# Four attention and mixture-of-experts layers on one core: expert results scattered to token rows, read by plain loads, with a stepped end and a first batch that goes ahead

## The chip, the cores and the metric

The kernel runs on one core of a Trainium2 chip. The metric is the device time of one launch in microseconds (us). The engines are PE (matrix products and transposes), DVE, ACT and POOL (element-wise work; POOL also issues indirect DMAs), and SP, which only issues DMAs.

## The reference, cut to what matters

A state `x` of 2 x 512 tokens by 256 values goes through four layers. Each adds an attention to a context and then a mixture of experts. Everything is float32. In layers 2 and 3 every token goes to two of eight experts, and the two results are weighted and added (`_layernorm` stands ahead of each):

```python
x = x + _L2_xattn_ref(_layernorm(x), ctx_1024, ...)   # causal, 16 heads of 16
# layer 2, experts: 2 of 8, gates = softmax over the two logits
for e in range(NUM_EXPERTS):
    h = jax.nn.relu(jnp.einsum('bsd,fd->bsf', x, w1[e]))
    y = jnp.einsum('bsf,df->bsd', h, w2[e])
    out = out + combine[..., e, None] * y
x = x + _L3_xattn_ref(_layernorm(x), ctx_1024, ...)   # rotary, 16 heads of 16
# layer 3, experts: 2 of 8, on h = rmsnorm(x @ W_in.T, in_norm_w)
for e in range(Wg.shape[0]):
    oe = rmsnorm(jax.nn.silu(h @ Wg[e].T) * (h @ Wu[e].T) @ Wd[e].T, enorm_w[e])
    out = out + gates[:, e:e + 1] * oe
s_hat = rmsnorm(out, out_norm_w) @ W_out.T
```

Layers 0 and 1 send each token to one expert. The kernel computes a token only in the experts it goes to.

## The kernel before

The 1024 tokens are `TT = 8` tiles of 128 (partition = token). `X`, 128 x 8 x 256, holds the state on the chip all the time. Tiles 0 to 3 are batch 0, 4 to 7 batch 1.

**Experts (`moe`).** `slots_of` gives every pick of a token a slot: a row of the DRAM tensor `xd`. Slots come in tiles of 128, each tile for one expert: one tile per expert (`s < 8`) and further ones for what overflows. For each pick and each token tile POOL issues an indirect DMA that scatters the 128 rows to their slots (L415; 16 of them in layers 2 and 3). Then `slot_tile(s)` runs for each tile: it loads the expert's weights `w` (a plain load by SP, L429, for `s < 8`; a gather by POOL, L431, beyond; `bufs=4`, so the load for tile s waits until tile s-4 is done with its weights), the rows `xs` (SP, L438), turns them (PE, L446; copy to `sT` on DVE, L448), multiplies (L132, L456 to L463), multiplies again into `y` (L466), and `finish` writes `yo`: a copy on ACT in layer 2 (`plain`, L480), a root-mean-square scaling on ACT and DVE in layer 3 (`normalise`, L1470). ACT then stores `yo` to the rows of the tile's slots in `yd` (L469). 19 tiles always run in layer 2 and 21 in layer 3 (`ALWAYS`); the rest stand in a `tc.If` on the counted number of tiles, which is a branch on each engine (L474). In the profiled execution it isn't taken in these layers.

**Combine.** For each token tile and each pick POOL gathers the rows of `yd` that the tile's tokens need (L487), and DVE multiplies by the gate and adds (L494, L496), into `X` in layer 2, into `acc` in layer 3. A gather waits for the stores of `yd`. In layer 3 follow, for all eight token tiles: `rms` (sums of squares on ACT, one root, eight scalings on DVE, L1449), the transposes (`to_T`, L117, copies on ACT, L122), the product with `w_out` (`po`, L132), the add into `X` (L1487) and the store (L1488).

**Attention of layers 2 and 3 (`attend16`).** Keys and values were computed before (`ahead16`, into the DRAM tensors `kd` and `vd`; L512, L557 to L562) and `fetch` loads them. `into_xT` normalises all of `X` (statistics L72, L73; `recip_sqrt`, L61 to L63; L98), turns it (L1190, copies alternately on ACT and DVE, L185 and L183) and adds the output bias to `X` (`add_bias`, L179). `prep(n)` makes the queries of group n (four heads of one batch; groups 0 to 3 are batch 0), `rotate` (L147 to L149) turns the keys in layer 3. After that comes a stream of slots whose order on PE is written out (`pe_in_order`): scores for the row maxima (`first_pass`, L1210, the maxima on DVE, L1216 or L1220), and, ten or more slots behind, scores again with the maxima taken off (`second_pass`, L1267, exponentials on ACT, L1268) and the products with the values. `Pieces` is a list of generators that are advanced a step at a time between slots; it holds the queries of the next group and the output products.

**What sets the order.** Code is written in program order, and a scheduler then orders each engine's instructions by readiness and program order and adds the waits; it may move an instruction ahead of others. What `keep` or `pe_in_order` marks stays in order. Instructions in a `tc.If` aren't mixed with those outside. Each engine works through its own list in order, and a waiting instruction holds those behind it.

`fill_slots` writes zeros to `xd` and to the tiles of `yd` that the branch may skip, during layer 0's attention.

Of the kernel before, what the change touches and what calls it, by code (L numbers as in the profile page):

```python
# [10 lines left out]
F32 = mybir.dt.float32  # L11
I32 = mybir.dt.int32
AF = mybir.ActivationFunctionType
ALU = mybir.AluOpType
# [3 lines left out]
P = 128  # L18
# [15 lines left out]
def tile_kernel(ctx: ExitStack, tc: tile.TileContext, d: dict, out: bass.AP):  # L34
# [369 lines left out]
    def moe(L, ps, hp, ep, rows, slots, wrow, used, F, act, glu, finish, filler=None):  # L404


        n_over = wrow.shape[1]
        NS = E + n_over
        FT, W1 = F // P, (2 * F if glu else F)
        xd, yd = xds[L]  # L410

        put = []
        for si in slots:
# [12 lines left out]
        def slot_tile(s):  # L426
# [41 lines left out]
            finish(yo, y, w)  # L468
            nc.scalar.dma_start(yd[s * P : (s + 1) * P, :], yo)  # L469

# [10 lines left out]

    def combine(hp, yd, slots, gates, dst, first):

        for t in range(TT):
            for i, si in enumerate(slots):
                yg = hp.tile([P, D], F32, tag="yg", name="yg", bufs=8)
                nc.gpsimd.indirect_dma_start(  # L487
                    out=yg, out_offset=None, in_=yd, in_offset=bass.IndirectOffsetOnAxis(ap=si[:, t : t + 1], axis=0)
                )
                to = dst[:, t, :]  # L490
                if gates is None:
                    nc.vector.tensor_add(to, to, yg)
                elif first and i == 0:
                    nc.vector.tensor_scalar(to, yg, gates[i][:, t : t + 1], None, ALU.mult)  # L494
                else:
                    nc.vector.scalar_tensor_tensor(to, yg, gates[i][:, t : t + 1], to, ALU.mult, ALU.add)  # L496
# [101 lines left out]
    def fill_slots(ins):  # L598

        zeros = const.tile([P, D], F32, tag="zeros", name="zeros")  # L600
# [5 lines left out]
        for L, NS in (("L0", 15), ("L1", 15), ("L2", 23), ("L3", 23)):  # L606
            xds[L] = [dram.tile([NS * P, D], F32, tag=f"{L}{n}d", name=f"{n}d") for n in "xy"]
            for to in xds[L][0], xds[L][1][(E + ALWAYS[L]) * P :, :]:
                nc.gpsimd.dma_start(
                    to.rearrange("(s p) f -> p s f", p=P), zeros[:, None, :].to_broadcast([P, to.shape[0] // P, D])  # L610
                )
# [4 lines left out]

    def normed(pool, twice, tag="xn"):
        xn = pool.tile([P, TT, D], F32, tag=tag, name="xn")
        layernorm(xn, X, TT, twice)
        return xn  # L620
# [3 lines left out]
    with (  # L624
# [31 lines left out]
        c_iota = route[:, 120:240].rearrange("p (s e) -> p s e", e=E)  # L656
        c_base, c_first, c_part = route[:, 240:248], route[:, 248:256], route[:, 256:257]

        nc.gpsimd.tensor_scalar(sin, sin, sign[:, 0:1], None, ALU.mult)
# [216 lines left out]
    with (  # L876
# [27 lines left out]
        ahead1(ps, hp, wkv, cT, 1)  # L904
        combine(hp, yd, slots, [mp], X, False)

# [207 lines left out]
    def attend16(L, params, nkt, causal, rotary, bias):  # L1114
# [11 lines left out]
        with (  # L1126
# [56 lines left out]

            def into_xT():
                xn = normed(cp, False, "oT1")
                for blk in range(TT // 4):
                    for dc in range(2):
                        pt = bank("pt")
                        for i in range(4):
                            nc.tensor.transpose(  # L1190
                                pt[:, i * P : (i + 1) * P], xn[:, blk * 4 + i, dc * P : (dc + 1) * P], ident
                            )
                        copy_alt(dc, xT[:, dc, blk * 512 : (blk + 1) * 512], pt)
                add_bias(bo)
# [168 lines left out]
    with (  # L1363
# [28 lines left out]
        ahead16(ps, fp, "L2", params, 4)  # L1392
        combine(hp, yd, slots, None, X, False)

# [4 lines left out]
    with (  # L1399
# [6 lines left out]
        xT = fp.tile([P, 2, NT], F32, tag="xT", name="xT")  # L1406
        xn = normed(fp, False)
        to_T(ps, xT, xn, TT)
# [15 lines left out]
    with (  # L1424
# [16 lines left out]

        def rms(t, w):

            ss = small.tile([P, TT], F32, tag="ss8", name="ss8")
            for i in range(TT):
                mean_squares(ss[:, i : i + 1], t[:, i, :])
            r = recip_sqrt(ss, TT, 1.0 / D, RMS_EPS)
            for i in range(TT):
                nc.vector.scalar_tensor_tensor(  # L1449
                    t[:, i, :], t[:, i, :], r[:, i : i + 1], w, ALU.mult, ALU.mult  # L1450
                )

        xT = fp.tile([P, 2, NT], F32, tag="xT", name="xT")
        to_T(ps, xT, normed(fp, False), TT)
        h = fp.tile([P, TT, D], F32, tag="h", name="h")
        for t in range(TT):
            ph = ps.tile([P, D], F32, tag="mm", name="ph")
            mm2(ph, xT, slice(t * P, (t + 1) * P), w_in, slice(0, D))
            nc.scalar.copy(h[:, t, :], ph)
        rms(h, inw)  # L1460
        hnT = fp.tile([P, 2, NT], F32, tag="hnT", name="hnT")
# [19 lines left out]
        aT = fp.tile([P, 2, NT], F32, tag="xT", name="aT")  # L1481
        to_T(ps, aT, acc, TT)
        outv = out.flatten_outer_dims()
        for t in range(TT):
            po = ps.tile([P, D], F32, tag="mm", name="po")
            mm2(po, aT, slice(t * P, (t + 1) * P), w_out, slice(0, D))
            nc.vector.tensor_add(X[:, t, :], X[:, t, :], po)  # L1487
            nc.sync.dma_start(outv[t * P : (t + 1) * P, :], X[:, t, :])  # L1488

# [49 lines left out]
def _route():  # L1539

    e = np.arange(E, dtype=np.float32)
    row = np.concatenate([
# [5 lines left out]
    ]).astype(np.float32)  # L1548
    return np.concatenate([np.tile(row, (P, 1)), np.arange(P, dtype=np.float32)[:, None]], axis=1)

# [105 lines left out]
```

## Time and profile before

| | us |
|---|---|
| median of 3 runs (2302.83 to 2308.51) | 2302.84 |
| the profiled execution | 2307.93 |
| its span, first to last instruction | 2306.2 |
| PE busy / share of the span | 2094.5 / 91% |
| DVE busy / share | 1070.3 / 46% |
| ACT busy / share | 863.9 / 37% |
| POOL busy / share | 439.8 / 19% |
| layer 1's end and layer 2's first queries | 1222 to 1258 |
| layer 2's slot tiles behind the key work | 1480 to 1622 |
| layer 2's end and layer 3's first queries | 1622 to 1664 |
| layer 3's attention | 1664 to 1950 |
| layer 3's slot tiles | 2022 to 2263 |
| layer 3's end | 2263 to 2306 |

All times inside the span count from its first instruction. A row of the timeline gives start, duration, engine, line, operation, the tile written and those read, shapes, how many instructions are merged into it, and in brackets the idle time of the engine before it with what ended it. `SPq`, `ACTq` and `POOLq` are DMA issues and other instructions that don't count as busy. A float32 product appears as two matmuls, a transpose as one.

### The profile page before, as it was taken

The page shows a single profiled execution, that of the slowest core. Times are in us where ns is not written, and L with a number is a line of the kernel's source. Part 1 is how long each engine was busy: PE and PEld are TensorE (multiplying, and loading weights), DVE is VectorE, ACT ScalarE, POOL GpSimd, SP SyncE. Part 2 cuts the span into 40 slices and gives each one's busy share as a digit, 9 for nine tenths or more (in the row PEclk, how much of TensorE's full clock was granted, in tenths as well). Part 3 has the DMA queues.
Part 4 walks back from the last instruction along what each step waited for, and adds up shares of the span by engine and source line. Part 5 has one row for each costly group of instructions (what it writes and reads, how often), then busy time and mean ns, then how long its engine had stood idle before and what let it go on. Part 6 is the DMA issues. An engine that isn't in the chain of part 4 may idle for free. (4 is left out here: it accounts for less than half of the span.)

```text
span 2306.2 us, 30582 instructions
## 1 busy us (share of the span) xinstructions
PE 2094.5 (91%) x11892; PEld 1274.1 (55%) x11892; DVE 1070.3 (46%) x2017; ACT 863.9 (37%) x1652; POOL 439.8 (19%) x418
## 2 busy tenths in 40 slices
PE   7899999989998999998998998899399999489994
PEld 3344444459974445544685344699243333489993
DVE  7566666641125565555214772000477773212222
ACT  4344444431115655554111332312035555234332
POOL 3233222210012112111101221200423310200002
PEclk9999999999999999999898997999689999689997
DMA  6511111277844011003274115686311101557851
GB/s 189 174 33 42 33 29 31 88 273 277 308 147 137 28 37 37 28 1 123 86 256 137 34 30 228 239 310 241 106 51 47 34 15 70 212 214 308 325 221 60
DMA packets 105766, 301.93 MB, mean 131 GB/s; under 512 B 23504, under 2 KB 67792, under 8 KB 96912
## 3 DMA queue, kind: packets, MB, share of 16 engines
q1 hardware_dynamic: 72400, 155.57, 19.7%
q0 software_dynamic: 12384, 114.70, 13.4%
q10 hardware_dynamic: 20832, 29.63, 3.5%
q8 instruction: 98, 1.61, 0.3%
q14 instruction: 52, 0.43, 0.1%
HBM read 243.39 MB, written 48.41 MB: 127 GB/s over the span
## 5 line engine op out<-in xcount | busy, mean ns | idle before, releaser
L1268 ACT ACTIVATE p<-s 128x512 f32<-128x512 f32 (+3 forms) x384 | 185.9, 545 | 191.4 <-PE s L1267 130.5
L132 PE MATMUL pa<-sT,w 128*128 128x128 f32 x1920 | 236.2, 278 | 12.1 <-DVE sT L448 3.7
L132 PEld LDWEIGHTS pa<-sT,w 128*128 128x128 f32 x1920 | 227.4, 193 | 20.6 <-ACT sq L1440 5.8
L1210 PE MATMUL s<-kT,qT 32*128 32x512 f32 (+3 forms) x768 | 216.7, 612 | 13.1 <-POOL kT L149 6.1
L466 PE MATMUL y<-w,hT 128*128 128x256 f32 x960 | 219.6, 381 | 3.9 <-DVE hT L463 3.1
L1267 PE MATMUL s<-qA,kT 32*128 32x512 f32 (+3 forms) x768 | 198.8, 595 | 1.0 <-ACT p L1268 0.7
L466 PEld LDWEIGHTS y<-w,hT 128*128 128x128 f32 x960 | 177.3, 190 | 27.9 <-DVE hT L463 4.4
L1220 DVE TENSOR_REDUCE mx<-s 128x1 f32<-128x512 f32 x256 | 163.1, 684 | 54.4 <-PE s L1210 34.2
L463 DVE TENSOR_TENSOR hT<-act,pg 128x512 f32<-128x512 f32 x82 | 56.3, 688 | 266.3 <-PE pg L132 225.1
L132 PE MATMUL pg<-sT,w 128*128 128x128 f32 x1312 | 160.8, 276 | 1.0 <-ACT sv L529 1.0
L819 ACT ACTIVATE p<-s 128x1024 f32<-128x1024 f32 x128 | 124.2, 1021 | 98.1 <-PE s L814 98.0
L978 ACT ACTIVATE p<-s,nm 128x512 f32<-128x512 f32 x192 | 129.3, 685 | 82.8 <-DVE nm L975 82.8
L132 PEld LDWEIGHTS pg<-sT,w 128*128 128x128 f32 x1312 | 154.0, 193 | 1.2 <-ACT sv L529 1.2
L975 DVE TENSOR_REDUCE nm<-s 128x2 f32<-128x1024 f32 x96 | 113.2, 1221 | 81.9 <-PE s L971 81.8
L820 DVE TENSOR_SCALAR p<-p 128x1024 f32<-128x1024 f32 x128 | 106.6, 840 | 89.9 <-ACT p L819 89.9
L149 POOL TENSOR_TENSOR kT<-kT,turned 128x512 f32<-128x512 f32 x62 | 100.9, 1632 | 217.9 <-DVE turned L147 208.5
L448 DVE COPY sT<-pt 128x256 f32<-128x256 f32 x66 | 25.6, 419 | 246.1 <-PE pt L446 246.1
L745 PE MATMUL o<-p,v 128*64 128x512 f32 x512 | 126.4, 610 | 10.3 <-DVE p L820 10.3
L825 DVE TENSOR_TENSOR acc<-acc,p 128x1024 f32<-128x1024 f32 x96 | 133.8, 1394 | 2.8
L814 PE MATMUL s<-qT,kT 64*128 64x512 f32 x512 | 128.4, 620 | 0.0
L431 POOL DMA_INDIRECT w<-in_L_experts_dram,wrow x34 | 32.3, 950 | 501.5 <-PE pt L446 124.9
L1210 PEld LDWEIGHTS s<-kT,qT 32*128 32x128 f32 x768 | 78.2, 190 | 68.6 <-issue 26.1
(274 smaller groups left out, 3077.8 us busy)
## 6 DMA issues: line engine op xcount, KB each, us to landing
w<-in_L_experts_dram SPq DMA_DIRECT2D x8, 3200.0 KB
w<-in_L_experts_dram SPq DMA_DIRECT2D x8, 3072.0 KB
w<-in_L_experts_dram SPq DMA_DIRECT2D x8, 2048.0 KB
w<-in_L_experts_dram SPq DMA_DIRECT2D x8, 1536.0 KB
kd<-sk ACTq DMA_DIRECT2D x40, 256.0 KB
xs<-xd SPq DMA_DIRECT2D x66, 128.0 KB
yd<-yo ACTq DMA_DIRECT2D x66, 128.0 KB
kT<-kd SPq DMA_DIRECT2D x16, 512.0 KB
```

The source lines that it names most:

```text
L132: nc.tensor.matmul(ps_ap, lhsT[:, dc, lcols], rhs[:, dc, rcols], start=(dc == 0), stop=(dc == 1))
L466: nc.tensor.matmul(y, hT[:, f, :], w2[:, f, :], start=(f == 0), stop=(f == FT - 1))
L745: nc.tensor.matmul(G[n]["o"][64 * j : 64 * j + 64, :], V[g, b][:, kt, pr * P + 64 * j : pr * P + 64 * j + 64], p[:, j, :], start=(kt == 0) ...
L814: nc.tensor.matmul(s1[:, j, :], G[n]["kT"][r, kt * P : (kt + 1) * P], G[n]["qT"][r, :], start=True, stop=True)
L819: nc.scalar.activation(p, s1, AF.Exp, scale=0.125)
L825: nc.vector.tensor_add(G[n]["acc"], G[n]["acc"], p)
L975: nc.vector.tensor_reduce(nm[:, qt, :, c], s1, AX.X, ALU.max, negate=True)
L978: nc.scalar.activation(p[:, j, :], s1[:, j, :], AF.Exp, bias=nm[:, qt, j, c : c + 1], accum_out=l[:, qt, j, c : c + 1],)
L1210: nc.tensor.matmul(s1[:, :w], qT[r, qt * P : (qt + 1) * P], kT[r, c * 512 : c * 512 + w], start=True, stop=True)
L1220: nc.vector.tensor_reduce(mx[:, qt, j, c : c + 1], s1, AX.X, ALU.max)
L1267: nc.tensor.matmul(s2[:, qs], kT[r, kt * P : (kt + 1) * P], qA[r, qs], start=True, stop=True)
L1268: nc.scalar.activation(p[:, j, qs], s2[:, qs], AF.Exp, scale=0.25)
```

## The change

Four edits:

1. **Names travel with the rows.** In layers 2 and 3 the rows scattered to `xd` get a 257th value: the token's number `c_tok` (0 to 1023) for the first pick, `c_tok + 1024` for the second, written by DVE (one copy, and eight small adds between the scatters). Unused slots are filled with `2048 + partition`. `c_tok` is eight further columns of the constant `route`.
2. **Scatter instead of store.** Each slot tile turns its names into row numbers (three small DVE instructions) and POOL scatters `yo` to rows of `yd`: rows 0 to 1023 hold the first picks by token, 1024 to 2047 the second, and behind them lies a row for each unused slot (2048 + 128 s + partition). ACT's store goes in these layers. `yd` isn't filled with zeros there any more.
3. **Plain loads and steps.** `combine2` reads whole token tiles of `yd` with loads by SP: in layer 2 four tiles of one pick per load (four loads, batch 0 first), in layer 3 two tiles per load. Layer 3's end runs in four steps of two token tiles, each from the loads to the store. Layers 0 and 1 keep gathers and `combine`.
4. **One batch first.** In `attend16` (layers 2 and 3) the statistics, the normalising and the transposes are done for batch 0, then the first queries; the statistics of batch 1 are written ahead of the stream, and its normalising, transposes and the bias add become a generator in `Pieces`.

The diff's core:

```diff
@@ moe
+        named = len(slots) == 2
+        RW = D + named
+        for i, si in enumerate(slots):
+            if named and i == 0:
+                nc.vector.tensor_copy(rows[:, :, D], c_tok)
             for t in range(TT):
+                if i == 1:
+                    nc.vector.tensor_scalar(rows[:, t, D:], c_tok[:, t : t + 1], float(NT), None, ALU.add)
                 x = nc.gpsimd.indirect_dma_start(
...
-            xs = hp.tile([P, D], F32, tag="xs", name="xs", bufs=4)
+            xs = hp.tile([P, RW], F32, tag="xs", name="xs", bufs=4)
...
-            nc.scalar.dma_start(yd[s * P : (s + 1) * P, :], yo)
+            if not named:
+                nc.scalar.dma_start(yd[s * P : (s + 1) * P, :], yo)
+                return
+            to = hp.tile([P, 2], F32, tag="to", name="to", bufs=3)
+            nc.vector.tensor_scalar(to[:, 0:1], xs[:, D:], 2.0 * NT, float(s * P), ALU.is_ge, ALU.mult)
+            nc.vector.tensor_add(to[:, 1:2], to[:, 0:1], xs[:, D:])
+            ti = hp.tile([P, 1], I32, tag="ti", name="ti", bufs=3)
+            nc.vector.tensor_copy(ti, to[:, 1:2])
+            x = nc.gpsimd.indirect_dma_start(
+                out=yd, out_offset=bass.IndirectOffsetOnAxis(ap=ti[:, 0:1], axis=0), in_=yo, in_offset=None
+            ).ins
+            for y in out_of:
+                tc.declare_no_dep(x, y, reason="rows of different tokens")
+            out_of.append(x)
@@
+    def combine2(hp, yd, gates, dst, t0, n, first):
+
+        for i in range(2):
+            yg = hp.tile([P, n, D], F32, tag="yg", name="yg", bufs=4)
+            r0 = i * NT + t0 * P
+            nc.sync.dma_start(yg, yd[r0 : r0 + n * P, :].rearrange("(t p) f -> p t f", p=P))
+            for t in range(n):
+                to, g = dst[:, t0 + t, :], gates[i][:, t0 + t : t0 + t + 1]
+                if first and i == 0:
+                    nc.vector.tensor_scalar(to, yg[:, t, :], g, None, ALU.mult)
+                else:
+                    nc.vector.scalar_tensor_tensor(to, yg[:, t, :], g, to, ALU.mult, ALU.add)
@@ fill_slots
-            for to in xds[L][0], xds[L][1][(E + ALWAYS[L]) * P :, :]:
+            for to in xds[L][:1] if RW > D else (xds[L][0], xds[L][1][(E + ALWAYS[L]) * P :, :]):
@@ attend16
-            def into_xT():
-                xn = normed(cp, False, "oT1")
...
+            def into_xT(b):
+
+                for dc in range(2):
+                    pt = bank("pt")
+                    for i in range(4):
+                        nc.tensor.transpose(pt[:, i * P : (i + 1) * P], xn[:, b * 4 + i, dc * P : (dc + 1) * P], ident)
+                    copy_alt(dc, xT[:, dc, b * 512 : (b + 1) * 512], pt)
+                    yield
+
+            def second_batch(norm):
+                norm_to(xn, X, norm)
+                yield
+                yield from into_xT(1)
                 add_bias(bo)
...
-            into_xT()
+            norm_to(xn, X, norm_of(X, 0, 4))
+            for _ in into_xT(0):
+                pass
...
             pieces = Pieces()
+            pieces.add(second_batch(norm_of(X, 4, 4)), 3)
@@ layer 2
-        combine(hp, yd, slots, gates, X, False)
+        for b in range(B):
+            combine2(hp, yd, gates, X, 4 * b, 4, False)
@@ layer 3
-        combine(hp, yd, slots, gates, acc, True)
-
-        rms(acc, onw)
...
+        for t0 in range(0, TT, 2):
+            combine2(hp, yd, gates, acc, t0, 2, True)
+            rms(acc, onw, t0, 2)
+            pt = ps.tile([P, 2, 2, P], F32, tag="mm", name="pt")
+            for dc in range(2):
+                for i in range(2):
+                    nc.tensor.transpose(pt[:, dc, i, :], acc[:, t0 + i, dc * P : (dc + 1) * P], ident)
+            aT = hp.tile([P, 2, 2 * P], F32, tag="aT", name="aT")
+            nc.scalar.copy(aT, pt.rearrange("p c i f -> p c (i f)"))
+            po = ps.tile([P, 2, D], F32, tag="y", name="po")
+            for i in range(2):
+                mm2(po[:, i, :], aT, slice(i * P, (i + 1) * P), w_out, slice(0, D))
+            nc.vector.tensor_add(X[:, t0 : t0 + 2, :], X[:, t0 : t0 + 2, :], po)
+            nc.sync.dma_start(outv[:, t0 : t0 + 2, :], X[:, t0 : t0 + 2, :])
```

The other lines of the diff widen `xn` and `h` by one column, let `rms` take two token tiles, and add the eight columns to `_route`.

More of the change, by code (lines that the diff above doesn't have):

```diff
@@ L410, in moe @@
         xd, yd = xds[L]
-        put = []
-        for si in slots:
+        put, out_of = [], []
+        named = len(slots) == 2
[3 more added lines that the diff above has]
+                nc.vector.tensor_copy(rows[:, :, D], c_tok)
             for t in range(TT):
+                if i == 1:
+                    nc.vector.tensor_scalar(rows[:, t, D:], c_tok[:, t : t + 1], float(NT), None, ALU.add)
                 x = nc.gpsimd.indirect_dma_start(
@@ L480, in plain, with combine @@
         nc.scalar.copy(yo, y)
-    def combine(hp, yd, slots, gates, dst, first):
+    def combine2(hp, yd, gates, dst, t0, n, first):
[9 more added lines that the diff above has]
+                    nc.vector.scalar_tensor_tensor(to, yg[:, t, :], g, to, ALU.mult, ALU.add)
+    def combine(hp, yd, slots, gates, dst):
         for t in range(TT):
@@ L492, in combine @@
                     nc.vector.tensor_add(to, to, yg)
-                elif first and i == 0:
-                    nc.vector.tensor_scalar(to, yg, gates[i][:, t : t + 1], None, ALU.mult)
                 else:
@@ L598, in fill_slots @@
     def fill_slots(ins):
-        zeros = const.tile([P, D], F32, tag="zeros", name="zeros")
+        zeros = const.tile([P, D + 1], F32, tag="zeros", name="zeros")
         z = nc.gpsimd.memset(zeros, 0.0).ins
@@ L605, in fill_slots @@
         )
-        for L, NS in (("L0", 15), ("L1", 15), ("L2", 23), ("L3", 23)):
-            xds[L] = [dram.tile([NS * P, D], F32, tag=f"{L}{n}d", name=f"{n}d") for n in "xy"]
-            for to in xds[L][0], xds[L][1][(E + ALWAYS[L]) * P :, :]:
+        nc.gpsimd.tensor_scalar(zeros[:, D:], c_part, 2.0 * NT, None, ALU.add)
+        for L, NS, RW in (("L0", 15, D), ("L1", 15, D), ("L2", 23, D + 1), ("L3", 23, D + 1)):
+            rows = NS * P + (2 * NT if RW > D else 0)
+            xds[L] = [
+                dram.tile([NS * P, RW], F32, tag=f"{L}xd", name="xd"), dram.tile([rows, D], F32, tag=f"{L}yd", name="yd")
+            ]
+            for to in xds[L][:1] if RW > D else (xds[L][0], xds[L][1][(E + ALWAYS[L]) * P :, :]):
                 nc.gpsimd.dma_start(
-                    to.rearrange("(s p) f -> p s f", p=P), zeros[:, None, :].to_broadcast([P, to.shape[0] // P, D])
+                    to.rearrange("(s p) f -> p s f", p=P),
+                    zeros[:, None, 0 : to.shape[1]].to_broadcast([P, to.shape[0] // P, to.shape[1]]),
                 )
@@ L615, in psum, with normed @@
         return tc.tile_pool(name=name, bufs=tags, space=PSUM, reuse_waits="tile")
-    def normed(pool, twice, tag="xn"):
-        xn = pool.tile([P, TT, D], F32, tag=tag, name="xn")
-        layernorm(xn, X, TT, twice)
+    def normed(pool, twice, tag="xn", width=D):
+        xn = pool.tile([P, TT, width], F32, tag=tag, name="xn")
+        layernorm(xn[:, :, 0:D], X, TT, twice)
         return xn
@@ L657, in tile_kernel @@
         c_base, c_first, c_part = route[:, 240:248], route[:, 248:256], route[:, 256:257]
+        c_tok = route[:, 257:265]
         nc.gpsimd.tensor_scalar(sin, sin, sign[:, 0:1], None, ALU.mult)
@@ L904, in tile_kernel @@
         ahead1(ps, hp, wkv, cT, 1)
-        combine(hp, yd, slots, [mp], X, False)
+        combine(hp, yd, slots, [mp], X)
     with (
@@ L1182, in prep @@
                 yield
-            def into_xT():
-                xn = normed(cp, False, "oT1")
[L1186 to L1193, printed above, removed]
+            xn = cp.tile([P, TT, D], F32, tag="oT1", name="xn")
+            def into_xT(b):
[9 more added lines that the diff above has]
+                yield from into_xT(1)
                 add_bias(bo)
@@ L1392, in tile_kernel @@
         ahead16(ps, fp, "L2", params, 4)
-        combine(hp, yd, slots, None, X, False)
+        combine(hp, yd, slots, None, X)
     attend16("L2", params, 4, True, False, True)
@@ L1406, in tile_kernel @@
         xT = fp.tile([P, 2, NT], F32, tag="xT", name="xT")
-        xn = normed(fp, False)
+        xn = normed(fp, False, width=D + 1)
         to_T(ps, xT, xn, TT)
@@ L1440, in mean_squares, with rms @@
             nc.scalar.activation(sq, src, AF.Square, accum_out=ss)
[L1442 to L1448, printed above, removed]
+        def rms(t, w, t0, n):
+            ss = small.tile([P, n], F32, tag=f"ss{n}", name="ss")
+            for i in range(n):
+                mean_squares(ss[:, i : i + 1], t[:, t0 + i, 0:D])
+            r = recip_sqrt(ss, n, 1.0 / D, RMS_EPS)
+            for i in range(n):
                 nc.vector.scalar_tensor_tensor(
-                    t[:, i, :], t[:, i, :], r[:, i : i + 1], w, ALU.mult, ALU.mult
+                    t[:, t0 + i, 0:D], t[:, t0 + i, 0:D], r[:, i : i + 1], w, ALU.mult, ALU.mult
                 )
@@ L1454, in tile_kernel @@
         to_T(ps, xT, normed(fp, False), TT)
-        h = fp.tile([P, TT, D], F32, tag="h", name="h")
+        h = fp.tile([P, TT, D + 1], F32, tag="h", name="h")
         for t in range(TT):
@@ L1458, in tile_kernel @@
             mm2(ph, xT, slice(t * P, (t + 1) * P), w_in, slice(0, D))
-            nc.scalar.copy(h[:, t, :], ph)
-        rms(h, inw)
+            nc.scalar.copy(h[:, t, 0:D], ph)
+        rms(h, inw, 0, TT)
         hnT = fp.tile([P, 2, NT], F32, tag="hnT", name="hnT")
@@ L1477, in tile_kernel @@
         acc = fp.tile([P, TT, D], F32, tag="acc", name="acc")
-        combine(hp, yd, slots, gates, acc, True)
-        rms(acc, onw)
[L1481 to L1488, printed above, removed]
+        outv = out.flatten_outer_dims().rearrange("(t p) f -> p t f", p=P)
+        for t0 in range(0, TT, 2):
[12 more added lines that the diff above has]
+            nc.sync.dma_start(outv[:, t0 : t0 + 2, :], X[:, t0 : t0 + 2, :])
 def _rotary_table(n, dim, pitch):
@@ L1548, in _route @@
     ]).astype(np.float32)
-    return np.concatenate([np.tile(row, (P, 1)), np.arange(P, dtype=np.float32)[:, None]], axis=1)
+    p = np.arange(P, dtype=np.float32)[:, None]
+    return np.concatenate([np.tile(row, (P, 1)), p, p + 128.0 * np.arange(TT, dtype=np.float32)], axis=1)
 def _experts(w1, w2, extra=None):
```

## The prediction, made before the changed kernel ran

> **What bounds the kernel now.** The page gives PE 91% of a 2306.2 us span, so most of the span can't move: PE works on. I read first the table of busy time by stage, to find where it doesn't, then the chain of waits for the end, then the timeline rows. In the table the columns are the stretch, its length, busy time of PE, PEld, DVE, ACT and POOL, PE clock, DMA share, GB/s:
>
> ```profile
> 1222.00:1251.00 29.00, 23.97 (x64) 13.96 (x64) 10.18 (x35) 6.88 (x10) 8.91 (x10) 0.88 0.48 168
> 1480.00:1622.00 142.00, 138.14 (x930) 127.40 (x930) 6.47 (x17) 30.45 (x58) 10.41 (x11) 1.00 0.71 262
> 1622.00:1651.00 29.00, 0.33 (x2) 0.15 (x1) 12.05 (x37) 1.86 (x3) 18.29 (x20) 0.54 0.37 113
> 1651.00:1664.00 13.00, 6.72 (x22) 4.24 (x22) 9.02 (x13) 1.76 (x3) 5.36 (x4) 0.76 0.53 164
> 1664.00:1700.00 36.00, 33.71 (x103) 15.89 (x104) 27.55 (x49) 4.11 (x7) 10.72 (x9) 0.70 0.23 73
> 2022.00:2263.00 241.00, 233.08 (x1722) 220.87 (x1722) 52.40 (x126) 93.17 (x147) 12.33 (x13) 0.98 0.65 255
> 2263.00:2306.00 43.00, 11.95 (x48) 9.56 (x48) 14.15 (x35) 6.52 (x21) 15.25 (x16) 0.64 0.25 77
> ```
>
> The slot tiles (1480 to 1622, 2022 to 2263) are PE's. The two stretches behind them (1622 to 1651, 2263 to 2306) are nobody's: a chain runs through 16 gathers. Layer 1's end (1222 to 1251) looks the same in the code, but there PE has the key work of `ahead16`. The chain that ended last (start, us, what) shows the 43 us:
>
> ```profile
> 2263.49 1.93 DMA yd<-yo
> ...
> 2266.43 0.96 POOL yg L487
> 2267.39 0.30 issue
> 2267.70 0.96 POOL yg L487
> ...
> 2284.05 2.55 DMA yg<-yd,si
> ...
> 2294.92 7.94 PE po L132 x32
> ```
>
> One gather every 1.26 us (0.96 + 0.30), then all of PE's work behind the last. POOL's issuing is what the change takes out.
>
> **Layer 3's end.** Removed: the ACT write, 16 gathers, the step from all tokens to PE. Added: one scatter, eight 256 KB loads, four steps. Scatter: POOL starts 0.28 us (cast of si ends 1999.90, scatter 2000.18) to 0.77 us (yo ends 2219.01, gather 2219.78) after its release; I take 0.5. From the last xd scatter's start to SP's dependent load is 2.41 us (2019.36 to 2021.77), and that load reaches PE 2.19 us later. 128 KB more at the 300 GB/s that the busy slices show is 0.44. So: yo ends 2263.45 + 0.5 + 2.41 + 2.19 + 0.44 = 2269.0 for the first combine; before it was 2269.27. The wait is neither gained nor lost; what follows is.
>
> Before, 2306.2 - 2269.3 = 36.9 us followed. After, DVE is the tightest. Per step: two products 0.35, two multiply-adds 0.485, rsq 0.17, reciprocal 0.20, two scalings 0.41 (L1449, 3.26 for eight), one add of 128x512, 0.69 (as L1179) = 3.55 us; four steps 14.2, and 1.5 for hand-overs that nothing fills. Behind the last scaling come four transposes (2.06/8 each, 1.0), a copy 0.59, two po (0.86 apart, 1.7) = 3.3, and the store: 2303.3 to the span's end 2306.2 is 2.9, 0.44 more for twice the bytes. Together 14.2 + 1.5 + 3.3 + 3.3 = 22.3. The loads of steps 3 and 4 wait for yg buffers (4); they start when steps 1 and 2 have multiplied, about 2270.4 and later, and land some 2.7 us on, while DVE is in step 2. Gain 36.9 - 22.3 + 0.3 = **15 us**. Bounds: 11 (loads land one behind the other, DVE idles once per step), 18 (no gaps).
>
> **Layer 2's end and layer 3's first batch.** The rows (start, us, engine, line, operation):
>
> ```profile
> 1622.25 0.37 ACT L480 COPY yo<-y 128x256 f32<-128x256 f32 x1 [2.86 <-PE y L466]
> 1629.32 0.48 DVE L496 SCALAR_TENSOR_TENSOR X<-yg,sel,X 128x256 f32<-128x256 f32 x1 [14.45 <-DMA yg<-yd,si]
> 1647.55 0.48 DVE L496 SCALAR_TENSOR_TENSOR X<-yg,sel,X 128x256 f32<-128x256 f32 x1 [0.38 <-DMA yg<-yd,si]
> 1650.88 3.80 PE L1190 MATMUL pt<-ident,xn 128*128 128x128 f32 x16 [28.67 <-DVE xn L98]
> 1653.62 2.28 DVE L179 TENSOR_TENSOR X<-X,bo 128x2048 f32<-128x2048 f32 x1
> 1678.30 10.70 PE L1210 MATMUL s<-kT,qT 32*128 32x512 f32 x30 [0.87 <-DVE mx L1220]
> ```
>
> The first combine stands where it was: 1622.62 + 0.5 + 2.41 + 2.19 + 1.3 (384 KB more) = 1629.0. A 512 KB load takes 1.75 us at 300 GB/s, four multiply-adds 0.44 each back to back = 1.76, so loads and DVE keep pace: batch 0 is whole at about 1632.6, batch 1 at 1636. Batch 0's statistics (four of 0.40) share DVE with batch 1's multiply-adds, which come first in the code; then rsq, square root, reciprocal and the first xn, 1.4 us. First transpose between 1635.5 (statistics first) and 1639 (multiply-adds first); I take 1637.3, 13.5 us earlier. Eight transposes less save 0.9 more before pq (DVE's copy of the second half then sets it). The kT and turned loads stood behind yg's buffers (v is issued at 1648.06, as the last X ends) and move along. Gain at the first score: 14.4.
>
> Given back: the second batch's four xn (1.34), its DVE copy (0.69) and the add of bo (2.28), 4.3 us, now stand in the first group of scores, where the row at 1678.30 shows PE waiting for the maxima on DVE (27.55 of 36 us busy). I count 3 of the 4.3, since DVE idles about 1.5 us at 1668 to 1672. Bounds 0 and 4.3. Net **11.4 us**, from 7 to 16. In 1700 to 1950 PE is full and hides nothing more, but nothing more is added there.
>
> **Layer 1's end.** The gathers stay. Batch 0 is whole four gathers earlier, but PE is in ahead16 until 1249.6. Its one hole (1236.4 to 1239.66) comes from ACT, which holds the key copies behind the square root at 1238.56; a root for batch 0 alone could come earlier, the second may hold ACT as before. Gain 0.8 to 4; in the first group DVE again gets up to 4.3 us more. I take **0**, from -4 to +4.
>
> **The tile loops.** Each of 40 tiles gets three DVE instructions of one column (0.15 as L61), 18 us in all, on a DVE that is busy 6.5 of 142 and 52 of 241 us; they read xs, which lands tiles ahead. Cover gone, they would stand before sT's copies, for which PE waits 0.3 to 0.5 us: at most 18. ACT loses 0.33 us of issuing per tile, hidden anyway. Rows of 1028 B in xd: nearest row the scatters of 1024 B, bound by issue (1.27 us apart), so 0, at most 1 per layer. Zero fills: two fewer, under layer 0's attention, 0. The name column of slot 1 waits for the scatter of slot 0 of the same tile, 10 us before it on POOL: 0. New waits: on POOL the scatter waits for yo, with the next weight gather behind it (a rival below) and, at layer 2's end, the branch and the memsets of nm and turned (L1137, 2.9 us, at 1645.7 before, so earlier now); on SP the yg loads wait for the last scatter, with v and turned of layer 3's attention behind them, which needed yg's buffers anyway. The branch on POOL now stands behind the last scatter; its INC_SWDGE_SEM lasted 0.63 to 1.91 us, beside the scatter's own 2.4: 0, at most 1 per layer. I book **-0.4** for all of these.
>
> A rule against the change: the scatters' spacing holds beside DVE work here (longest DMA_INDIRECT of yg 1.21 us where the median is 0.95). The Trainium skill, SBUF — State Buffer, section "SBUF: two separate sides", says GpSimd can't write descriptors while DVE holds the shared ports, and advises the other queues. By its example (about 620 ns grown to 3100, section "A bandwidth-pool intuition that's wrong (but worth ruling out)") my estimate is 2.5 us per scatter; two of them are on the path, and the sum would be 21 instead of 26. The row decides: 0.3 us.
>
> **Sum.** 15 + 11.4 + 0 - 0.4 = 26. The profiled execution took 2307.93 us (1.7 around its span), so 2281.9; the runs' median lies 5.1 below it, at 2302.84: **2277**.
>
> **Rivals.**
> - Only the end gains. Batch 1's combine goes first and its 4.3 us per layer is all lost: 11 + 7 - 4 = 14, so 2289.
> - Everything gains: 18 + 16 + 4 = 38, so 2265. For it: ACT's stall in layer 1 is in plain sight; against it, DVE's full first group.
> - It doesn't do what it says: the loads wait for something else (the branch's semaphores, buffers still held), gains 0 to 7, so about 2299. For it only that SP's queue is shared.
> - Slower: POOL's order. Weight gathers and scatters now share POOL. In the code a tile's scatter stands ahead of the next tile's gather. A scheduler reorders (the memset of L547 runs at 1399.55, ahead of scatters that precede it in the code), and a gather comes free with the tile whose scatter is due, so I expect pairs:
>
> ```profile
> 2219.78 0.94 POOL L431 DMA_INDIRECT w<-in_L_experts_dram,wrow  x1 [10.68 <-DVE yo L1474]
> ```
>
> These weights are used at 2249.88. 3.28 MB at 320 GB/s is 10.2, and 2.4 to start: the gather may slip by 17.5 us, past one scatter (tile 17's yo, 2229.6), not past two (2241.2). Past two it would start at 2243.0 (1.8 us for scatter and start), 5.7 late, for each of 13 tiles of layer 3; by the same sum in layer 2 (2.1 MB; 1592.38, used at 1614.92, third yo 1607.57) 3.3 for each of 11: 110 us, 84 after the gains: 2387.
>
> **Numbers.** Forecast 0.56; only the end 0.18; everything 0.13; not as it says 0.06; POOL's order 0.07. The range takes the first three: 2264 to 2291. A measurement here tells about 0.3% (7 us) from no change; so faster 0.86, same 0.06, slower 0.08.
>
> **What would show it.** Right: no gathers behind 2263, four groups of DVE work with po among them; the first transpose of layer 3's attention 15 us after the last yo instead of 28; POOL's rows in pairs of gather and scatter, tiles still 7.5 and 11.1 us apart. Wrong: PE waiting for w in the tile loops, SP's yg loads long after the last scatter, or the first scores of layers 2 and 3 with gaps as long as what the lead-in lost.

## The result and the profile after

| | before | changed |
|---|---|---|
| median, us | 2303.19 (8 runs, 2302.04 to 2309.77) | 2312.84 (8 runs, 2308.22 to 2319.79) |
| profiled execution, us | 2307.93 | 2314.39 |
| its span, us | 2306.2 | 2312.7 |

The ratio is 1.0038 with a 95% interval of 1.0021 to 1.0056: **slower** by 0.4%, where 26 us of gain were forecast. The two profiled spans differ by +6.5 us. Cut at events that both kernels have, that is (for a `yo` the start of the instruction that writes it, for layer 1's last `yo` the issue of its store; sums are off by rounding):

| stage (from the event before to this one) | before | changed | difference |
|---|---|---|---|
| start to layer 1's last `yo` | 1221.4 | 1229.4 | +8.0 |
| to layer 2's first scatter into `xd` | 227.1 | 225.6 | -1.5 |
| to layer 2's last `yo` (the tiles) | 173.7 | 175.3 | +1.6 |
| to layer 3's first scatter into `xd` (layer 2's end, layer 3's attention) | 377.9 | 368.5 | -9.4 |
| to layer 3's last `yo` (the tiles) | 262.8 | 285.8 | +23.0 |
| to the end of the span | 43.2 | 28.1 | -15.1 |

So layer 3's end gave what was forecast, and layer 3's tiles took it back and more. The table of busy time by stretch of the changed kernel, columns as in the prediction (stretch, length, PE, PEld, DVE, ACT, POOL, PE clock, DMA share, GB/s):

```profile
1487.00:1630.00 143.00, 137.54 (x928) 126.87 (x926) 12.98 (x61) 29.81 (x57) 28.32 (x29) 1.00 0.70 258
1631.00:1651.00 20.00, 0.00 (x0) 0.00 (x0) 10.56 (x38) 1.61 (x3) 3.71 (x5) 0.56 0.55 184
2022.00:2263.00 241.00, 221.59 (x1587) 206.38 (x1588) 54.87 (x178) 85.09 (x134) 30.35 (x31) 0.96 0.65 253
2263.00:2285.00 22.00, 18.83 (x137) 17.39 (x135) 4.56 (x11) 8.09 (x14) 1.93 (x2) 1.00 0.05 15
2285.00:2312.00 27.00, 12.69 (x48) 9.65 (x48) 12.61 (x37) 6.55 (x24) 0.97 (x1) 0.68 0.38 122
```

In the same 241 us from 2022 on PE is busy 221.59 instead of 233.08 us (1587 matmuls instead of 1722), and it needs 22 us more to finish. The stretch that was empty behind layer 2 is 20 us long instead of 29, and the one behind layer 3 is 27 instead of 43.

What PE waits for in layer 3's tiles, from the table of waits of the changed kernel (engine, line waited for: us in total, times, longest); the 27.5 us is the start:

```profile
PE pt L455 <- DMA xs<-xd: 27.5, 1, 27.5
PE y L475 <- DVE hT L472: 15.2, 7, 3.5
```

In the kernel before, these are the only two waits of PE there, so the wait for hT is new:

```profile
PE pt L446 <- DMA xs<-xd: 27.3, 1, 27.3
PE pa L132 <- ACT sq L1440: 3.7, 10, 0.6
```

The same table for DVE in the changed kernel:

```profile
DVE ti L485 <- DMA yd<-yo,ti: 57.1, 18, 6.9
...
DVE to L482 <- DMA xs<-xd: 32.4, 8, 12.1
```

DVE, on the way to hT, stands at the cast of a tile's row numbers (`ti`) until an earlier tile's scatter has landed. One tile of the timeline shows how (start, us, engine, line, operation, in brackets the idle time before it and what ended it):

```profile
2039.64 0.48 DVE L1523 SCALAR_TENSOR_TENSOR yo<-y,rsq,w 128x256 f32<-128x256 f32 x1
2040.40 0.97 POOL L486 DMA_INDIRECT yd<-yo,ti  x1 [21.47 <-DVE yo L1523]
2048.84 0.15 DVE L485 CAST ti<-to 128x1 int32<-128x1 f32 x1 [6.86 <-DMA yd<-yo,ti]
2048.92 0.69 DVE L472 TENSOR_TENSOR hT<-act,pg 128x512 f32<-128x512 f32 x1
2049.66 3.66 PE L475 MATMUL y<-w,hT 128*128 128x256 f32 x8 [3.47 <-DVE hT L472]
```

The scatter that starts at 2040.40 lands 8.4 us later, beside a weight load; the cast waits for it 6.86 us, the multiply `hT` (L472) stands behind the cast, and PE waits 3.47 us for hT. In DVE's instruction list the cast of tile k stands between `yo` of tile k-3 and `yo` of tile k-2. `ti` has 3 buffers, so that cast overwrites the row numbers of the scatter of tile k-3, whose `yo` was only just written.

The waits of PE for hT sum to 15.2 us, and the loop lost 23. Most of the rest is time in which PE works more slowly: its matmuls of this loop take 221.59 + 18.83 = 240.4 us by the rows above, against 233.1 before. The last row of the tile shows it: eight matmuls right behind the wait take 3.66 us, where the median of this instruction is 0.379 us each, and the stretch behind the wait has a granted PE clock of 0.55:

```profile
2049.60:2053.40 3.80, 3.74 (x11) 2.99 (x12) 0.01 (x1) 0.04 (x1) 0.00 (x0) 0.55 0.02 7
```

The chain that ended last shows layer 3's end as it was forecast, 2.42 us from the scatter to SP's load and then a plain load in place of 16 gathers:

```profile
2285.41 2.41 DMA yd<-yo,ti
...
2287.83 0.38 SPq L509
...
2288.77 3.67 DMA yg<-yd
...
2301.90 2.15 PE po L132 x8
...
2305.05 3.73 PE po L132 x16
```

At layer 2's end the same chain is longer:

```profile
1630.97 4.98 DMA yd<-yo,ti
1635.96 4.22 DMA yg<-yd
1640.18 0.03 issue
1640.21 1.46 DVE X L515 x4
...
1641.80 1.67 DVE X L515 x4
...
1643.80 0.86 DVE X L515 x3
...
1644.90 2.06 DVE X L515 x5
...
1651.05 1.47 PE pt L1231 x5
```

From the scatter to the load are 4.98 us, not 2.41. The scatter itself lands later than the 2.41 us that were taken: POOL waits for it at its branch until 1634.63, 3.66 us after its start. Then an instruction of the branch on POOL, INC_SWDGE_SEM, lasts 1.35 us, and SP's load starts as it ends. And DVE combines both batches (sixteen L515) before the first batch's statistics are done, so the first transpose (L1231) comes 20.4 us after the last `yo` ended, not 14.7.

### The profile page after: what moved, and what is told of

It reads as the page before. It is cut to its first block, busy times and chain, and to the rows that moved or that the text cites. A ratio compares the mean times of both kernels' runs of the same rounds, so it can differ in the third digit from the quotient of the medians.

```text
span 2312.7 us, 30736 instructions
## 1 busy us (share of the span) xinstructions
PE 2103.1 (91%) x11892; PEld 1272.0 (55%) x11892; DVE 1090.2 (47%) x2161; ACT 864.2 (37%) x1657; POOL 448.2 (19%) x425
## 5 line engine op out<-in xcount | busy, mean ns | idle before, releaser
L475 PE MATMUL y<-w,hT 128*128 128x256 f32 x960 | 226.2, 387 | 20.2 <-DVE hT L472 18.3
L472 DVE TENSOR_TENSOR hT<-act,pg 128x512 f32<-128x512 f32 x82 | 56.3, 687 | 208.8 <-PE pg L132 178.8
L1288 PE MATMUL o<-p,v 128*32 128x256 f32 (+3 forms) x1280 | 107.0, 406 | 6.7 <-POOL p L1317 6.4
L1032 PEld LDWEIGHTS pt<-ident,p 128*128 128x128 f32 x768 | 85.6, 140 | 49.3 <-issue 23.8
```

The lines of the kernel that those rows point to most:

```text
L475: nc.tensor.matmul(y, hT[:, f, :], w2[:, f, :], start=(f == 0), stop=(f == FT - 1))
L1288: nc.tensor.matmul(G[n]["o"][32 * j : 32 * j + 32, qs], G[n]["v"][:, kt, g % 2 * 4 + j, :], p[:, j, qs], start=(kt == 0 and half != 1), st ...
```

## Theories

1. DVE is held by the reuse of `ti`: its order puts the cast so early that it waits for a scatter just issued, and hT waits behind it. Either the place in the order (1a) or the number of buffers (1b) may be the cause.
2. POOL's order of scatters and weight gathers delays the weights (the prediction's slower rival).
3. `to`, which reads `xs`, waits for rows that land late.
4. Beginning attention with one batch gains nothing: because batch 1's combine goes first (4a), or because what is put off only moves into the stream (4b).
5. The +8 us of layers 0 and 1, where the transfers differ only in `fill_slots`, come from the fill of layers 2 and 3 in rows of 1028 B, from where the data lie, or are spread from one execution to the next.

## The experiments

Ratios are to the kernel before, with 95% intervals; "tiles" are the stage of layer 3's tiles in the table above (262.8 before, 285.8 changed).

**The kernel before, again** (no edit).

> The kernel before once more, for the spread of its stages. If the 8 us by which the changed kernel is late at layer 1's last yo (1229.4 against 1221.4) come from the wider zero rows and the other DRAM layout, this profile has layer 1's last yo at 1221 +- 2 again; if they are the spread from one execution to the next, it lies elsewhere between 1214 and 1230. Time 2302 to 2310, ratio 1.000.

Ratio 1.0006 (0.9992 to 1.0019). Layer 1's last `yo` is stored at 1227.5, against 1221.4 in the first profile of the same kernel: this stage spreads by 6 us from execution to execution, so +8 between two profiles shows nothing yet. The later stages repeat closely: tiles 262.7, end 43.1.

**More buffers for the row numbers.**

```diff
-            to = hp.tile([P, 2], F32, tag="to", name="to", bufs=3)
+            to = hp.tile([P, 2], F32, tag="to", name="to", bufs=24)
-            ti = hp.tile([P, 1], I32, tag="ti", name="ti", bufs=3)
+            ti = hp.tile([P, 1], I32, tag="ti", name="ti", bufs=24)
```

> The changed kernel with 24 buffers for to and ti in place of 3, so that DVE's cast never has to wait for an earlier tile's scatter to have read its row numbers. Theory 1 (DVE, in order, is held by that reuse, and hT behind it holds PE): the waits of ti for yd<-yo,ti are gone, layer 3's tiles take about 241 us from the first xs to the last yo as in the kernel before instead of 263, layer 2's gain a few us, and the time falls by 20 to 26 to about 2288 (2284 to 2294). Theory 2 (the order of scatters and weight gathers on POOL): nothing changes, 2311 to 2316. Theory 3 (to waits for the rows xs, which land late): the waits move from ti to to, and at most 8 us come back, 2304 to 2309.

Ratio 0.9942 (0.9928 to 0.9957), median 2292.07, some 21 us less than the changed kernel; tiles 266.3 instead of 285.8. Theory 2 falls: POOL still issues scatter and gather in pairs, and nothing is late. Theory 1 holds for the most part, and some of theory 3 is left, 3.5 us: with more buffers the scheduler puts the row numbers even further ahead, up to five tiles, and the rows of DVE's waits and of one tile in this run read

```profile
DVE to L482 <- DMA xs<-xd: 39.0, 10, 11.9
```

```profile
2214.82 0.15 DVE L482 TENSOR_SCALAR to<-xs 128x1 f32<-128x1 f32 x1 [6.20 <-DMA xs<-xd]
2214.92 0.48 DVE L1523 SCALAR_TENSOR_TENSOR yo<-y,rsq,w 128x256 f32<-128x256 f32 x1
...
2216.33 3.72 PE L475 MATMUL y<-w,hT 128*128 128x256 f32 x16 [1.77 <-DVE hT L472]
```

The row number of a later tile waits 6.20 us for that tile's rows, and this tile's `yo` and hT wait behind it.

**The row numbers behind the tile's own work**, with 3 buffers as in the changed kernel.

```diff
-            nc.vector.tensor_copy(sT, pt)
+            last = nc.vector.tensor_copy(sT, pt).ins
...
-                nc.vector.tensor_mul(to, a, pg)
+                last = nc.vector.tensor_mul(to, a, pg).ins
...
-            nc.vector.tensor_scalar(to[:, 0:1], xs[:, D:], 2.0 * NT, float(s * P), ALU.is_ge, ALU.mult)
+            x = nc.vector.tensor_scalar(to[:, 0:1], xs[:, D:], 2.0 * NT, float(s * P), ALU.is_ge, ALU.mult).ins
+            tc.add_manual_dep(x, last.name, ...)
```

> The changed kernel, 3 buffers for to and ti as it has, with one dependency more: a tile's three row-number instructions stand behind its own last DVE instruction ahead of yo (hT in layer 3, sT in layer 2). In the changed kernel DVE's order has the cast of tile k between yo(k-3) and yo(k-2), so with 3 buffers it waits there for the landing of the scatter that was only just issued. Theory 1a (the place in DVE's order is the cause, not the number of buffers): the waits of ti for yd<-yo,ti go although there are 3 buffers, those of to for xs go too, layer 3 from its first xd scatter to its last yo takes 262 to 264 us (before 262.7, with 24 buffers 266.3, changed 285.8), time 2286 to 2291. Theory 1b (three buffers are too few in any order, since a scatter takes up to 8.5 us): 2305 or more.

Ratio 0.9925 (0.9911 to 0.9939); tiles 262.3. DVE's waits for the scatter and for xs are gone, and what PE waits for in these tiles is what it was before (27.3 and 3.7 us):

```profile
PE pt L455 <- DMA xs<-xd: 27.5, 1, 27.5
PE pa L132 <- ACT sq L1493: 3.7, 10, 0.6
```

```profile
2029.00:2270.00 241.00, 232.31 (x1722) 220.11 (x1722) 62.75 (x189) 93.22 (x147) 33.12 (x34) 0.99 0.66 255
```

DVE does all 63 row-number instructions (189 instead of 126, 10.35 us more busy than before) and PE has its 1722 matmuls in 241 us again. From layer 3's first `yo` to its last are 222.1 us, as in the kernel before; the changed kernel had 245.0 there and the kernel with 24 buffers 225.5. So 1a holds and 1b falls: three buffers are enough, and the three instructions cost this loop nothing, if they stand where their inputs are there and their buffer is free.

**The fill of layers 2 and 3 put off** (on top of the last kernel): `fill_slots` for layers 0 and 1 stays at step 5 of layer 0's attention, that for layers 2 and 3 goes to step 17.

```diff
-                fill_slots(G[1]["ready"])
+                fill_slots(G[1]["ready"], D)
                 add_bias(bo)
+            if t == 17:
+                fill_slots(G[4]["ready"], D + 1)
```

> The kernel e5_order with the fill of layers 2 and 3's rows (1028 B each, with their name) put off until group 4 of layer 0's attention, some 140 us on, where the DMA engines are 0.13 busy. Theory 5 (the fill in rows of 1028 B holds up layer 0's exchanges: 24.8 and 26.0 us to landing against 22.2, PE's product waits 9.9 and 10.9 us for DVE's p against 6.6 and 7.2): the product's wait before 115 us falls to 3 or less, layer 1's last yo comes 4 to 9 us earlier than in e5_order, time 2280 to 2286. Rival (the difference is spread, or the fill only collides with other exchanges later): within 2 of e5_order.

Ratio 0.9902 (0.9882 to 0.9923), 0.0023 less than without this edit, with intervals that overlap. Layer 1's last `yo` is stored at 1223.5 (1235.4 in the profile of the kernel without this edit, which is the latest of five with the early fill, 1229.4 to 1235.4). What PE waits for from 31 to 115 us, in the changed kernel and then in this one:

```profile
PE o L785 <- DVE p L860: 9.9, 3, 8.5
```

```profile
PE o L794 <- DVE p L869: 1.1, 1, 1.1
```

**The same edit on the kernel before**, to see whose collision that is.

> The kernel before with nothing but the fill of layers 2 and 3 put off to group 4 of layer 0's attention, as in e6_fill_late. If the whole collision with layer 0's exchanges is the fill's place, and its rows of 1028 B add only the difference (wait of PE's product for p 9.9 to 12.3 us in five profiles of the changed layout, 6.6 to 7.2 in two of before): the wait falls from about 7 to 1, and the kernel before gains 4 to 7, ratio 0.997 to 0.998. If the rows of 1028 B alone are the cause: ratio 0.999 to 1.000.

Ratio 0.9963 (0.9950 to 0.9976), layer 1's last `yo` at 1216.5, and this wait falls from 7.2 to 1.1:

```profile
PE o L745 <- DVE p L820: 7.2, 3, 5.9
```

```profile
PE o L746 <- DVE p L821: 1.1, 1, 1.1
```

So the collision is an old one that both kernels pay. The changed layout adds to it: the wait was 9.9 to 12.3 us in five of its profiles and 6.6 to 7.2 in three of the old layout, about 4 us more. The times alone can't show that part: putting the fill off brought 0.0023 there and 0.0037 here, and the intervals overlap. But layer 1's last `yo` also stays apart with the late fill, 1216.5 here, 1223.5 with the changed layout.

**Odd widths, and moved addresses.** Two more kernels ask whether that is where the data lie. The first is the kernel with order and fill mended and attention's beginning as before (the third at the end of this section) with

```diff
-    zeros = const.tile([P, D + 1], F32, tag="zeros", name="zeros")
+    zeros = const.tile([P, 320], F32, tag="zeros", name="zeros")
```

and `route` 320 columns wide as well; the second is the kernel before with the late fill, `zeros` 257 wide and

```diff
+            more = {"x": 12 + 2 * NT, "y": 0} if NS == 23 else {"x": 0, "y": 0}
-            xds[L] = [dram.tile([NS * P, D], F32, tag=f"{L}{n}d", name=f"{n}d") for n in "xy"]
+            xds[L] = [dram.tile([NS * P + more[n], D], F32, tag=f"{L}{n}d", name=f"{n}d") for n in "xy"]
```

> The kernel e10_no_first_fixed with the tiles of zeros and of route 320 columns wide in place of 257 and 265, nothing else: the tiles behind them lie on multiples of 256 B again, as in the layout before. If the odd widths make layers 0 and 1 slower (layer 1's last yo at 1223.5, 1225.1 and 1221.7 in three profiles with the late fill, 1216.5 in the old layout's one): about 1216 to 1218, and the ratio 0.985 to 0.987. If they don't: 1221 to 1226, and the ratio 0.987 to 0.991 as before.

> The kernel e9_before_fill_late with the addresses moved and no transfer changed: zeros 257 columns wide, and xd of layers 2 and 3 with 2060 unused rows behind its own, about what names and rows for unfilled slots added. If addresses make layers 0 and 1 slower: layer 1's last yo at 1221 to 1226 as in the changed layout, ratio 0.998 to 1.000. If not: 1216 to 1219 and a ratio near 0.996; if the first profile with the late fill was only on the fast end of a spread of 6 us, anything up to 1222 with the ratio near 0.996.

Ratios 0.9904 (0.9872 to 0.9936) and 0.9969 (0.9955 to 0.9982); layer 1's last `yo` at 1223.9 and 1216.0. Neither the odd widths nor addresses moved like this do it. With the late fill the old layout has 1216.5 and 1216.0, the changed one 1221.7 to 1225.1 in four profiles. One wait behind the late fill is longer there, PE's `po` for POOL's `oT`, 2.5 to 3.1 us against 0.9 to 1.5. The other 5 to 6 us build up through layers 0 and 1 in pieces of up to some 2 us, and no run places them.

**The second batch of layer 2's end put off.** Its loads, combine and statistics go into the pieces of layer 3's attention (`late` is `combine2` for batch 1), on top of the kernel with the order mended:

```diff
-            def second_batch(norm):
-                norm_to(xn, X, norm)
+            def second_batch():
+                if late is not None:
+                    late(cp)
+                    yield
+                norm_to(xn, X, norm_of(X, 4, 4))
```

> The kernel e5_order with the second batch's loads, combine and statistics of layer 2's end moved behind the first batch's transposes, into the pieces of layer 3's attention. Theory 4a (the forecast's 14.4 for this lead-in became 7.4 because DVE combines and takes statistics of batch 1 first): first transpose 14 to 16 us after layer 2's last yo instead of 21, and 3 to 6 us off the time, 2281 to 2287. Theory 4b (the DVE work only moves into the stream of first scores, where PE waits for it as long): the first transpose is early, and the time within 2 of e5_order.

Ratio 0.9942 (0.9926 to 0.9959), median 2293.89: no gain (0.9925 without this edit). Here is the first transpose and what follows on PE:

```profile
1641.24 2.10 PE L1235 MATMUL pt<-ident,xn 128*128 128x128 f32 x8 [15.75 <-DVE xn L98]
...
1654.40 2.09 PE L1262 MATMUL s<-kT,qT 32*128 32x512 f32 x8 [6.20 <-POOL kT L149]
...
1671.63 2.07 PE L1262 MATMUL s<-kT,qT 32*128 32x512 f32 x2 [3.45 <-DVE mx L1272]
1677.84 1.45 PE L1235 MATMUL pt<-ident,xn 128*128 128x128 f32 x4 [4.14 <-DVE xn L98]
```

The same places without this edit:

```profile
1656.31 2.10 PE L1235 MATMUL pt<-ident,xn 128*128 128x128 f32 x8 [21.35 <-DVE xn L98]
...
1681.02 0.66 PE L1235 MATMUL pt<-ident,xn 128*128 128x128 f32 x4 [0.84 <-DVE mx L1269]
```

The lead-in is about what the forecast took: 15.7 us from the start of the last `yo` to the first transpose (forecast 15, and 21.3 without this edit). But then PE waits 3.45 us for the maxima and 4.14 us for the second batch's `xn`, where it waited 0.84 us, and the whole stage takes 373.4 us against 371.2. Both parts of theory 4 are true: batch 1's combine is what delays the first transpose (4a), and putting it off only moves the wait (4b).

**Fill and second batch together.**

> The edits of e5_order, e6_fill_late and e7_second_late together. If both gains hold and add up: 2274 to 2281. If only one does: 2280 to 2287.

Ratio 0.9906 (0.9890 to 0.9921), stage 373.4: the fill's gain and nothing from the second batch.

**Attention's beginning, undone and alone.** Three kernels: the changed one with

```diff
-            norm_to(xn, X, norm_of(X, 0, 4))
-            for _ in into_xT(0):
-                pass
+            into_xT()
...
-            pieces.add(second_batch(norm_of(X, 4, 4)), 3)
```

(`into_xT` for both batches, as before), the kernel before with only the edit to `attend16`, and the kernel with order and fill mended without that edit.

> The changed kernel with attention's beginning as before (both batches normed and transposed ahead of the first scores). Theory 4 (beginning with one batch costs more than it gains, because DVE combines both batches first and the rest falls into the stream): faster than the changed kernel by 2 to 6, 2307 to 2311. If the beginning gains what the two traces show in layer 2 (28.3 us to the first transpose before, 20.4 after, some 1.6 lost in the stream, of which the combine in four steps holds a part): slower by 4 to 8, 2316 to 2321.

> The kernel before with attention's beginning of the changed kernel and nothing else of the change. By the traces of layer 1's end (gain 2.7 in the lead-in, 1.2 lost in the stream) and of layer 2's (with 16 gathers the second batch's rows come last, so the first batch's norm need not wait for them: 5 to 10 gained there): 2292 to 2299, faster by 3 to 10. Theory 4: 2302 to 2306, no gain.

> The kernel e6_fill_late with attention's beginning as before (both batches ahead of the first scores), to price that edit beside a loop that no longer stalls. Theory 4b (the second batch's work is only moved into the stream, where PE waits for it): within 3 of e6_fill_late, ratio 0.989 to 0.992. If beginning with one batch gains what the forecast's 11.4 took for it: 5 to 10 slower, ratio 0.993 or more.

Ratios 1.0057 (1.0040 to 1.0073; the changed kernel 1.0038), 1.0005 (0.9993 to 1.0018), and 0.9886 (0.9866 to 0.9905; with the edit 0.9902). Undoing it once looks worse and once better, each inside the intervals; alone it does nothing. Its price is 0 within about 0.2%. Its lead-in says the same: 20.9 to 21.9 us without it in three profiles, 20.7 to 21.6 with it in four. With the old combine it leaves the lead-in at 28.5 us, and the stage up to layer 3's first scatter takes 380.5 us, against 373.2 to 377.9 in four profiles without it. Two expectations failed here: 2307 to 2311 for the first kernel if theory 4 holds (its median is 2317.26), and a gain of 3 to 10 for the second.

The last of these kernels, with the row numbers in their place, the late fill and attention's beginning as before, has the lowest time of all, a median of 2281.08 us. Against the kernel before with the same late fill it is 0.9886/0.9963 = 0.992 (0.990 to 0.995, from the two intervals), and that is what the scatter and the plain loads are worth once they stall no tile loop; it still contains what the changed layout loses in layers 0 and 1.

## Why the prediction was wrong

**The tile loops: the step that failed.** The prediction wrote of the three DVE instructions that "they read xs, which lands tiles ahead", gave the bound "Cover gone, they would stand before sT's copies", and booked -0.4 for everything in the loops. It asked what the instructions read and how long they last, and not what they write: a buffer that comes free only when an earlier scatter has landed. The two facts that were needed were known, that a scheduler moves instructions ahead and that an engine works through its list in order, and it used them for POOL only. The loop lost 23.0 us between the two profiles; mending the order alone brings it from 285.8 to 262.3. PE's waits for hT are 15.2 us of it, and slower matmuls behind them some 7. The bound of 18 us, the sum of the instructions' own durations, was no bound either, since a wait isn't limited by the length of the instruction that waits. No rival had this mechanism; the slower one, POOL's order, fell: scatter and gather came in the pairs that it hoped for, and no `w` came late.

**Layer 2's tiles.** DVE waited even more there, and the stage lost 1.6 us:

```profile
DVE ti L485 <- DMA yd<-yo,ti: 74.2, 16, 12.2
```

In layer 2 hT is ACT's work, and DVE has only the sT copies behind the cast; PE waited for these 4.6 us in all, against 2.9 before. From layer 2's first `yo` to its last are 137.2 us, against 135.5 before and 135.5 again with the order mended. So a wait of 74.2 us on DVE cost 1.7 us, and one of 57.1 us in layer 3 cost 23: what stands behind the waiting instruction decides, and not the sum in the table of waits. With the order mended, the part ahead of layer 2's first `yo` takes 38.7 to 40.2 us in six profiles, against 37.2 to 38.2 in the others; the cause of this loss stays open.

**Layer 3's end.** Forecast 15, measured 15.1, and 14.3 to 15.8 in the other profiles (27.4 to 28.9 us instead of 43.2). The steps held: scatter to load 2.42 (2.41 taken). Step by step it went otherwise, and that the sum came out is partly luck: PE's last `po` and transposes are on the chain behind each other, where the prediction had DVE as the tightest. DVE's last scaling ends 12.5 us after the first combine starts (14.2 + 1.5 = 15.7 forecast), and 9.6 us follow it (3.3 + 3.3 = 6.6 forecast).

**Layer 2's end.** Forecast 14.4 at the first score less 3 given back, 11.4. Measured: the first score comes 34.5 us after the start of the last `yo` instead of 42.2, a gain of 7.7, and the stage gains 9.4 between the first two profiles. Over four profiles of the old combine and the old beginning of attention (377.9, 376.7, 373.2, 375.5) and four of both new ones (368.5, 372.9, 371.2, 371.9) the means differ by 4.7; three with the new combine and the old beginning (370.7, 367.4, 371.7) lie 5.9 below the old ones, so the gain is the combine's alone. Two terms were mis-sized. The load started 4.98 us after the scatter, not 2.41: the scatter was seen to land after 3.66, and 1.35 of the branch on POOL came behind it, where the prediction had put the branch "beside the scatter's own 2.4". And the multiply-adds of batch 1, and the statistics of both batches, stood ahead of the first `xn`; the prediction had weighed the first of these as its late bound, 16.4 us from the last `yo` to the first transpose, and with the 2.6 us by which the load was late that is 19.0 of the 20.4 measured. The run that put the second batch off shows that the forecast's lead-in was possible and its gain was not: DVE's work in front of the first scores has no cover there.

**Layer 1's end.** Forecast 0, measured -1.5 us in a stage that spreads from 221.6 to 227.1.

**Layers 0 and 1.** "Zero fills: two fewer, under layer 0's attention, 0" was wrong: PE waits there for an exchange through DRAM that the fill slows down, about 4 us more than before. The means of the early-fill profiles, 1224.6 over three of the old layout (1221.4, 1227.5, 1224.8) and 1231.2 over five of the changed one (1229.4, 1231.2, 1230.7, 1235.4, 1229.4), differ by 6.6; what makes up the rest stays open.

**What the trace could have told.** The prediction listed as a sign of failure "PE waiting for w in the tile loops". The sign that came was PE waiting for hT. It could have been asked for in the same way: name, for each added instruction, the instruction right behind it on its engine.

## What to carry to other kernels

An added instruction on an in-order engine costs what the instruction behind it waits: look for what it waits to read and for whose buffer it overwrites, and at which place of the engine's list the scheduler will put it, since one whose inputs are early is moved early. Tie small side work to the tile it belongs to: here three buffers then did what twenty-four didn't. Before a lead-in is shortened by putting work off, look whether the stretch that is to take it has an idle engine.

## What the runs showed of the hardware

- A scatter of 128 rows of 1 KB lands 2.4 us after its issue in the quiet end of layer 3, and up to 8.8 us after it beside weight loads of 3.28 MB in layer 3's tiles (median of these 21 scatters 3.5). The Trainium skill, "DMA: Bandwidth & Descriptors", section "Anatomy of one DMA — SWDGE (gpsimd) path", gives about 2.0 us plus the bytes at 436 GB/s; for 128 KB my estimate by it is 2.3, which agrees with the quiet case and not with the busy one, and it was the busy one that decided here.
- The two fills of `xd` for layers 2 and 3 in rows of 1028 B took 24.8, 25.6 and 26.0 us to land (the median of the two, in three profiles), and slices of 2.1 us in their second half moved 218 to 305 GB/s and 177 to 321 GB/s in two of these profiles, where the rows of 1024 B took 22.2 us at 315 to 344 GB/s. No run here separates the row's length from the rest of the layout.
- Behind a wait of 3.47 us, PE's matmuls ran at a granted clock of 0.55 for 3.8 us and took up to twice their time (8 in 3.66 us, at a median of 0.379 each): a short wait of PE costs more than its own length.
- POOL issued the scatters of layer 3's tiles in 967 to 984 ns while DVE worked through its own instructions; the slowing that the prediction weighed by a rule did not show.
